# Layers 2 and 3 of a four-layer network: each token's two expert outputs kept as two rows in DRAM, or added into one row by the DMA that sends them

## The chip, the cores and the metric

The kernel runs on one core of one Trainium2 chip, in one launch. The time is device microseconds from the start to the end of an execution, taken as the median of several. The profile shows one further execution with its engines: PE (TensorE, the matrix unit, with PEld its weight loads), DVE (VectorE), ACT (ScalarE), POOL (GpSimd) and SP (SyncE, which here does nothing but issue DMAs). All numbers are fp32.

## The reference

A batch of 4 x 512 = 2048 tokens of 256 features goes through four residual layers. Each layer is an attention-like part plus a feed-forward part, both of the normed (layers 0 to 2) or residual input. In layers 1, 2 and 3 the feed-forward part is a mixture of experts: a router picks a few experts per token, and the token's output is the weighted sum of those experts' outputs. Layer 1 has 32 experts, of which each token uses 4; layer 2 has 7 routed experts, 2 per token, beside a shared one; layer 3 has 8 experts, 2 per token. Cut to what the change touches:

```python
# layer 2 (expert_ffn: silu(x @ wg) * (x @ wu) / 8 @ wd)
scores, idx = jax.lax.top_k(probs, 2)
scores = scores / jnp.sum(scores, axis=-1, keepdims=True)
w = jnp.sum(jax.nn.one_hot(idx, 7) * scores[..., None], axis=-2)
for e in range(7):
    combined = combined + w[..., e:e + 1] * expert_ffn(x, r_gate[e], r_up[e], r_down[e])

# layer 3
top_logits, top_idx = jax.lax.top_k(logits, 2)
cw = jnp.zeros((T, 8)).at[jnp.arange(T)[:, None], top_idx].add(jax.nn.softmax(top_logits, axis=-1))
for e in range(8):
    h = jax.nn.silu(x @ w0[e]) * (x @ w1[e])
    out = out + cw[:, e:e + 1] * (h @ wo[e])

# every layer
x = x + attention(...) + experts(...)
```

The result is x after layer 3.

## The kernel before

The residual stream x stays in SBUF all the time, as 16 tiles of 128 tokens by 256 features. Tensors in DRAM serve only to bring tokens of one expert together and to send them back.

**Routing.** `dispatch` (L158) counts, for each token and expert, which place the token takes among that expert's tokens. Places come in blocks of 128, and a block belongs to one expert: 2048 x 2 / 128 + experts − 1 blocks, so 38 in layer 2 and 39 in layer 3. A block that is not full has empty places. The normed tokens are written to a DRAM tensor `rows`, one row per token: 256 features, the token's number, its two places and its two shares (a row has 272 numbers). `in_slot` names, for every place of every block, the token that stands there.

**A block.** Both layers run over the blocks in a pipeline of stages, each of which handles another block in one turn.

- fetch: SP loads the weights of the block's expert. In layer 3 these are three matrices of 512 KB (`w0`, `w1`, `wo`, 1.5 MB together), in layer 2 one packed piece of 384 KB. POOL issues an indirect DMA, the *gather* (`load_rows`, L294), which brings the 128 rows of the block's tokens to the tile `r`.
- features: `block_rows` (L300 to L317) works out on DVE, for each of the 128 rows, its share and the row it goes to. `mine` (L306) marks which of the token's two places is this one; `both` (L311, L312) is `mine` times the shares and `mine` times 0 or 2048; a reduction (L314) gives the share and the offset; the token's number is added (L315) and the sum is cut at `beyond` (L317), which sends empty places to spare rows. `block_features` turns the rows round on PE (`rt`, L325) and ACT copies them (`rT`, L327).
- hidden: the two matrices of the expert on PE (`g` L1742 in layer 3), Silu on ACT (L1748), the product on DVE (`h` L1749).
- output: the last matrix on PE (`o` L1755 in layer 3, L1107 in layer 2), then `send_back` (L330): ACT scales by the share (`y`, L333), and POOL issues an indirect DMA, the *scatter* (L334), from `y` to the rows `to` of the DRAM tensor `outs`.

`outs` has one row per token and choice: rows 0 to 2047 for the first choice, 2048 to 4095 for the second, then 128 spare rows per block. No row is written twice, and `no_order` (L276) tells the scheduler that these scatters need no order among themselves. So a scatter waits for its data and for a free place in its queue, not for other scatters to land.

**Collecting.** `collect` (L338) adds the outputs to x. For each of 8 pairs of token tiles it loads 256 KB for the first choice and 256 KB for the second (L345 with `load`, L356) and adds both on DVE (L351). These loads wait for all scatters to have landed. In layer 3 the stores of x to the output (`store_x`, L369) follow pair by pair, and the kernel ends with them. Layer 1 uses the same functions with four outputs per token.

**What sets the order.** The engines run their instructions in the order in which a scheduler put them at build time; POOL, SP and DVE each have one queue in order. In layer 2 the experts are worked off beside the gated attention: the last 8 of 32 attention units are run with the experts' stages between their steps, and the collecting stands in front of the last unit (L1059). That unit's steps are, in this order, `ke` (L1193), `pok` (L1240), `ok` (L1245), `okt` (L1249) with `mx`, `pv` on DVE and ACT (L1253 to L1256), `st` (L1189), `Wg` (L1216), and `pvt` (L1269). Layer 3 begins with its norms (`layer_norm3`, L1758) and routers, which need the collected x. Layer 3's attention is mixed into the first blocks of its experts; PE's order there is written out by hand. In the steady part of layer 3's experts, POOL's queue holds alternately the scatter of block t and the gather of block t+6.

**Start-up.** `expert_rows` (L140) makes `rows` and `outs` while the first weights are loaded on SP's queue.

Of the kernel before, what the change touches and what calls it, by code (L numbers as in the profile page):

```python
# [7 lines left out]
F32 = mybir.dt.float32  # L8
AF = mybir.ActivationFunctionType
ALU = mybir.AluOpType  # L10
AX = mybir.AxisListType
PSUM = bass.MemoryType.PSUM

P = 128
NB = 4
T = 512
D = 256
KD = D // P
NTILE = NB * T // P
# [23 lines left out]
class Ring:  # L43
# [17 lines left out]
    def tile(self, shape, dtype, tag, name, bufs=None):  # L61
        if tag not in self.places and self.pool is None:
            n = 1
            for d in shape[1:]:
                n *= d
            self.places[tag] = [self.base[:, self.free + i * n : self.free + (i + 1) * n] for i in range(bufs)]
            self.free += bufs * n
            assert self.free <= self.base.shape[1]
        if tag not in self.places:
            return self.pool.tile(shape, dtype, tag=tag, name=name, **({"bufs": bufs} if bufs else {}))  # L70
        i = self.turn.get(tag, 0)
        self.turn[tag] = i + 1
        ap = self.places[tag][i % len(self.places[tag])][: shape[0], :]
        if len(shape) == 3:
            ap = ap.rearrange("p (a b) -> p a b", b=shape[2])
        return ap


class Net:
# [57 lines left out]

    def expert_rows(self, name, experts, k, sent=False):  # L140

        blocks = NB * T * k // P + experts - 1
        rows = self.tc.dram_tile([blocks * P if sent else NB * T + 1, EXT], F32, name=f"{name}_rows")
        outs = self.tc.dram_tile([k * NB * T + blocks * P, D], F32, name=f"{name}_outs")
        if sent:
            self.load(
                rows.rearrange("(n p) d -> p n d", p=P), self.none.unsqueeze(1).to_broadcast([P, blocks, EXT])  # L150
            )
        else:
            self.load(rows[NB * T :, :], self.none[:1, :])
        return dict(
            name=name, experts=experts, ne=max(experts, 8), k=k, blocks=blocks, rows=rows, outs=outs, sent=sent
        )

    def dispatch(self, moe, rows, top, w, wk, pool, tag, keep=None):  # L158
# [104 lines left out]
    def experts_of_blocks(self, moe, end, tile, keep):  # L263

        nc = self.nc
        ne, k, blocks = moe["ne"], moe["k"], moe["blocks"]
        past, of = tile("past", blocks, ne), tile("of", blocks, 1, of=keep)
        nc.vector.tensor_scalar(past, end[:blocks, :], self.number[:blocks, 0:1], None, ALU.is_le)
        nc.vector.tensor_reduce(of, past, AX.X, ALU.add)
        nc.vector.tensor_scalar(of, of, float(moe["experts"] - 1), None, ALU.min)  # L270
        moe["of"], moe["expert"] = of, tile("expert", blocks, 1, dt=mybir.dt.int32, of=keep)
        nc.vector.tensor_copy(moe["expert"], of)
        moe["beyond"] = tile("beyond", P, blocks, of=keep)
        nc.vector.tensor_scalar(moe["beyond"], self.number[:, :blocks], float(k * NB * T), None, ALU.add)

    def no_order(self, group, inst):  # L276
# [23 lines left out]
    def block_rows(self, moe, t, n, r, wk):  # L300

        nc = self.nc
        k = moe["k"]

        mine = wk.tile([P, n, k], F32, tag="mine", name="mine")
        nc.vector.tensor_tensor(  # L306
            mine, r[:, :, D + 1 : D + 1 + k], self.number[:, t : t + n].unsqueeze(2).to_broadcast([P, n, k]),
            ALU.is_equal,
        )
        both = wk.tile([P, 2, n, k], F32, tag="both", name="both")  # L310
        nc.vector.tensor_tensor(both[:, 0], mine, r[:, :, D + 1 + k : D + 1 + 2 * k], ALU.mult)  # L311
        nc.vector.tensor_tensor(both[:, 1], mine, self.layers[:, :k].unsqueeze(1).to_broadcast([P, n, k]), ALU.mult)  # L312
        share = wk.tile([P, 2, n], F32, tag="share", name="share", bufs=8)
        nc.vector.tensor_reduce(share, both, AX.X, ALU.add)  # L314
        nc.vector.tensor_tensor(share[:, 1], share[:, 1], r[:, :, D], ALU.add)  # L315
        to = wk.tile([P, n], mybir.dt.uint32, tag="to", name="to", bufs=8)
        nc.vector.tensor_tensor(to, share[:, 1], moe["beyond"][:, t : t + n], ALU.min)  # L317
        return share[:, 0], to

# [10 lines left out]
    def send_back(self, moe, ps, to, share, wk):  # L330
        nc = self.nc
        y = wk.tile([P, D], F32, tag="y", name="y", bufs=5)
        nc.scalar.activation(y, ps, AF.Copy, scale=share)  # L333
        self.no_order(moe["name"] + " back", nc.gpsimd.indirect_dma_start(  # L334
            out=moe["outs"][:, :], out_offset=bass.IndirectOffsetOnAxis(ap=to, axis=0), in_=y, in_offset=None
        ))

    def collect(self, moe, wk):  # L338

        for i in range(0, NTILE, 2):  # L340
            x = self.x[:, i : i + 2, :]
            ys = []
            for m in range(moe["k"]):
                y = wk.tile([P, 2, D], F32, tag="sum", name="sum", bufs=8)
                s = (m * NTILE + i) * P  # L345
                self.load(y, moe["outs"][s : s + 2 * P, :].rearrange("(n p) d -> p n d", p=P))
                ys.append(y)
            if len(ys) > 2:
                self.nc.gpsimd.tensor_tensor(ys[0], ys[0], ys.pop(), ALU.add)
            for y in ys[1:] + ys[:1]:  # L350
                self.nc.vector.tensor_tensor(x, x, y, ALU.add)  # L351
# [124 lines left out]
    def layer0(self):  # L476
        nc, a = self.nc, self.a
# [9 lines left out]
        with ExitStack() as ctx:  # L487
            tp = lambda n, bufs, **k: ctx.enter_context(self.tc.tile_pool(name=n, bufs=bufs, **k))
            wp, wk = tp("l0w", 1), tp("l0", 2)
# [10 lines left out]
            rows = wp.tile([P, 10, D], F32, tag="rows", name="rows")  # L500
# [14 lines left out]
            self.l1w = self.router1(32, routing)  # L515
            self.moe1 = self.expert_rows("l1", 32, 4, sent=True)
            self.packed_experts(self.moe1, "l1_w_gate", "l1_w_up", "l1_w_down")
            self.moe2, self.moe3 = self.expert_rows("l2", 7, 2), self.expert_rows("l3", 8, 2)
            self.packed_experts(self.moe2, "l2_r_gate", "l2_r_up", "l2_r_down")
            self.latent_ahead(early)  # L520
            self.weights = {0: self.gated_weights(0)}
# [101 lines left out]
            for b in range(NB):  # L623
                for c, g in enumerate(gates[b]):
# [5 lines left out]
                    for p in range(2):  # L630
                        y = g[:, p, :]
# [1327 lines left out]
```

## Time and profile before

| | |
|---|---|
| median of 3 runs | 2320.91 us (2320.03 to 2325.61) |
| profiled execution | 2334.37 us |
| its span | 2332.6 us |
| mean TensorE clock granted | 0.909 |
| PE busy | 2019.1 us (87%) |
| PE weight loads | 1501.4 us (64%) |
| DVE busy | 1240.0 us (53%) |
| ACT busy | 841.1 us (36%) |
| POOL busy | 625.8 us (27%) |
| scatters (L334), all layers | 172, 980 ns of POOL each |
| gathers (L294), layers 2 and 3 | 77, 1001 ns of POOL each |
| DMA over the span | 244.02 MB, mean 105 GB/s |

The profile page gives busy times over the whole span and in 40 equal slices; the trace behind it answers for any stretch of time what each engine did and what it waited for. A line such as `2245.14 0.99 POOL L334 DMA_INDIRECT l_outs<-y,to` reads: start and duration in us, engine, line of the kernel, operation, output and inputs; what stands in brackets is how long the engine had been idle before, and who ended that. For a DMA the duration on POOL or SP is that of issuing it; its data land later. `l_outs` stands for the `outs` of any layer, `we` for expert weights. Names like `xn<-l_outs` in the tail are the collecting loads of layer 3, into a buffer that is called `xn` there (`sum` in layer 2). The median of runs is 13.5 us below the profiled execution.

### The profile page before, as it was taken

Reading aid. Unit: us, or ns where it says so; the run is one execution under the profiler, and the core shown is the slowest. Engines: PE = TensorE matmul, PEld = TensorE weight load, DVE = VectorE, ACT = ScalarE, POOL = GpSimd, SP = SyncE. Lnnn points to the kernel's source line nnn. Section 1 sums busy time; section 2 is a strip of 40 time slices with the busy share of each in tenths; the row PEclk is TensorE's granted clock in tenths of the full one; section 3 lists DMA queues with packets and bytes.
Section 4 is the critical chain, followed back from the end, with each engine's and each line's share of the span. In section 5 each row is a group of like instructions: output and inputs, shape, how many; then the busy total and the mean of one; then the engine's idle time right before and its main releaser. Section 6 shows DMA issues by size and latency. Waiting matters only on the chain.

```text
span 2332.6 us, 36307 instructions
## 1 busy us (share of the span) xinstructions
PE 2019.1 (87%) x13455; PEld 1501.4 (64%) x13455; DVE 1240.0 (53%) x3682; ACT 841.1 (36%) x1729; POOL 625.8 (27%) x737
## 2 busy tenths in 40 slices
PE   6754088874999999999999999999999968899995
PEld 2453077762566676666766676656778755678995
DVE  5765056657655655565565656546555564422223
ACT  1110056552334443343344444332354413344221
POOL 5334634443111121111111121110444332012331
PEclk8855599996999999999999999998999977899998
DMA  9911378874000000000000000001433220166897
GB/s 314 331 42 58 108 271 280 281 255 146 1 8 10 6 12 6 5 17 6 4 14 5 8 10 5 8 10 39 133 113 110 86 79 19 61 224 237 291 330 242
DMA packets 152536, 244.02 MB, mean 105 GB/s; under 512 B 15846, under 2 KB 111944, under 8 KB 152232
## 3 DMA queue, kind: packets, MB, share of 16 engines
q1 hardware_dynamic: 137336, 199.50, 26.3%
q0 software_dynamic: 15024, 42.20, 5.2%
q8 instruction: 107, 1.75, 0.3%
q14 instruction: 69, 0.57, 0.1%
HBM read 190.41 MB, written 66.58 MB: 110 GB/s over the span
## 4 chain that ended last, share of the span: by engine, by line
PE 64%; DVE 12%; issue 10%; DMA 6%; POOL 5%; ACT 3%; SPq 1%; another core or an unknown queue 0%; POOLq 0%; DVEq 0%; ACTq 0%
PE pt L1216 7%; PE pj L1138 6%; PE g L1742 5%; PE o L1329 4%; PE kq L1551 3%; PE sc L1201 3%; PE pov L1280 2%; PE gu L959 2%; PE o L1755 2%; DMA r<-l_rows,in_slot 2%; PE qk L1519 2%; DVE junk L1526 2%; PE pv L1567 2%; DMA r<-l_rows 2%; PE qkp L1804 1%
## 5 line engine op out<-in xcount | busy, mean ns | idle before, releaser
L334 POOL DMA_INDIRECT l_outs<-y,to x172 | 168.5, 980 | 325.5 <-ACT y L333 243.2
L306 DVE TENSOR_TENSOR mine<-r,number 128x2 f32<-128x2 f32 (+1 forms) x96 | 15.5, 161 | 273.9 <-DMA r<-l_rows,in_slot 207.2
L294 POOL DMA_INDIRECT r<-l_rows,in_slot x77 | 77.1, 1001 | 276.9 <-PE rt L325 147.0
L1742 PEld LDWEIGHTS g<-rT,we 128*128 128x128 f32 x1248 | 145.2, 192 | 5.2 <-ACT rT L327 3.4
L1742 PE MATMUL g<-rT,we 128*128 128x128 f32 x1248 | 145.9, 275 | 2.4 <-ACT rT L327 2.4
L1526 DVE CUSTOM_DVE_ANT_0 junk<-qk,hide 128x512 f32<-128x512 f32 (+3 forms) x256 | 124.7, 487 | 43.5 <-PE qk L1519 24.9
L1559 POOL TENSOR_SCALAR_AFFINE_SELECT pr<-pr 128x512 f32<-128x512 f32 x64 | 40.2, 639 | 339.3 <-ACT pr L1556 339.3
L959 PE MATMUL gu<-rT,we 128*128 128x128 f32 x760 | 112.5, 287 | 21.4 <-issue 9.7
L325 PE MATMUL rt<-ident,r 128*128 128x128 f32 x344 | 67.1, 295 | 70.2 <-DMA r<-l_rows 69.0
L327 ACT COPY rT<-rt 128x256 f32<-128x256 f32 x172 | 62.6, 372 | 178.3 <-PE rt L325 103.1
L1329 PE MATMUL o<-Wo,oT 128*128 128x256 f32 x512 | 126.2, 390 | 0.0
L959 PEld LDWEIGHTS gu<-rT,we 128*128 128x128 f32 x760 | 104.3, 198 | 33.7 <-issue 16.3
L1216 PE MATMUL pt<-Wg,xnT 128*128 128x256 f32 x512 | 124.2, 394 | 1.3 <-PE ot L1322 0.5
L333 ACT ACTIVATE y<-o,share 128x256 f32<-128x256 f32 x172 | 81.2, 473 | 114.9 <-PE o L1755 48.1
L1207 DVE TENSOR_TENSOR s<-sc,keep 128x512 f32<-128x512 f32 x128 | 82.5, 684 | 72.4 <-PE sc L1201 72.3
L1216 PE MATMUL pt<-Wv,xnT 128*128 128x256 f32 x512 | 120.1, 385 | 0.0
L1151 DVE RECIPROCAL rz<-rz 128x128 f32<-128x128 f32 x128 | 117.5, 935 | 0.4
L1216 PEld LDWEIGHTS pt<-Wg,xnT 128*128 128x128 f32 x512 | 97.0, 195 | 26.0 <-issue 7.1
L413 PE MATMUL tr<-ident,xn 128*128 128x128 f32 x160 | 33.7, 357 | 85.8 <-DVE xn L398 81.3
L1216 PEld LDWEIGHTS pt<-Wv,xnT 128*128 128x128 f32 x512 | 95.0, 191 | 15.1 <-DVE st L387 0.2
L1556 ACT ACTIVATE pr<-kq 128x512 f32<-128x512 f32 (+1 forms) x192 | 86.2, 530 | 50.1 <-PE kq L1551 49.5
L325 PEld LDWEIGHTS rt<-ident,r 128*128 128x128 f32 x344 | 53.9, 203 | 77.6 <-issue 75.0
(457 smaller groups left out, 4565.1 us busy)
## 6 DMA issues: line engine op xcount, KB each, us to landing
we<-l_packed SPq DMA_DIRECT2D x133, 384.0 KB
we<-l_w SPq DMA_DIRECT2D x78, 512.0 KB
we<-l_wo SPq DMA_DIRECT2D x39, 512.0 KB
l_rows<-none SPq DMA_DIRECT2D x1, 12920.0 KB
r<-l_rows SPq DMA_DIRECT2D x19, 680.0 KB
xn<-l_outs SPq DMA_DIRECT2D x32, 256.0 KB
l_rows<-xn SPq DMA_DIRECT2D x8, 544.0 KB
l_packed<-l_w_gate SPq DMA_DIRECT2D x1, 4096.0 KB
```

What stands on the lines that cost most here:

```text
L325: nc.tensor.transpose(pt[:, k, :], r[:, :D].rearrange("p (d k) -> p k d", k=KD)[:, k, :], self.ident)
L333: nc.scalar.activation(y, ps, AF.Copy, scale=share)
L334: self.no_order(moe["name"] + " back", nc.gpsimd.indirect_dma_start(out=moe["outs"][:, :], out_offset=bass.IndirectOffsetOnAxis(ap=to, axi ...
L959: nc.tensor.matmul(ps[:, q, :], we[:, q, k * P : (k + 1) * P], rT[:, k, :], start=(k == 0), stop=(k == KD - 1))
L1138: nc.tensor.matmul(ps, w[n][:, k, :], self.xnT[:, k, t["b"] * T : (t["b"] + 1) * T], start=(k == 0), stop=(k == KD - 1))
L1151: inverse = lambda c: nc.vector.reciprocal(rz[:, c * P : (c + 1) * P], rz[:, c * P : (c + 1) * P])
L1207: nc.vector.tensor_tensor(s, ps[hh], keep4, ALU.mult)
L1216: nc.tensor.matmul(ps[:, i, :], self.xnT[:, k, s : s + P], w[n][:, k, :], start=(k == 0), stop=(k == KD - 1))
L1329: nc.tensor.matmul(ps[:, p, :], of_parity(oT[:, h, c * D : (c + 1) * D], p), wo[:, h, :], start=(h == 0), stop=(h == 1),)
L1526: nc.vector.tensor_tensor_reduce(out=junk[:, :m], in0=tiles[j][:, off : off + m], in1=self.hide[:, T - m :], op0=ALU.add, op1=ALU.max, sca ...
L1556: nc.scalar.activation(pr[:, j, off : off + m], tiles[j][:, :m], AF.Exp, scale=0.25)
L1742: nc.tensor.matmul(pt[:, m, :], we[:, q, k * T + m * P : k * T + (m + 1) * P], rT[:, k, :], start=(k == 0), stop=(k == KD - 1),)
```

## The change

For layers 2 and 3, `outs` has one row per token (2048) and 128 spare rows, in place of two rows per token and 128 spare rows per block. Two DMAs on SP's queue in the start-up fill each of these tensors, 2.23 MB, with zeros. The scatter becomes an indirect DMA that adds `y` to what the row holds. A token's row is now written by two scatters, and all blocks share the spare rows, so the scatters are no longer declared free of order: the scheduler puts a wait for the landing of the one before into each. The row to send to is the token's number itself, so two of the six DVE operations per block are gone. The collecting loads one tile per pair in place of two, and adds it: 8 loads and 8 additions in place of 16 and 16, in each of the two layers. Layer 1 stays as it was.

```diff
-    def expert_rows(self, name, experts, k, sent=False):
+    def expert_rows(self, name, experts, k, sent=False, added=False):
...
-        outs = self.tc.dram_tile([k * NB * T + blocks * P, D], F32, name=f"{name}_outs")
+        outs = self.tc.dram_tile([NB * T + P if added else k * NB * T + blocks * P, D], F32, name=f"{name}_outs")
+        if added:
+            n = NB * T // P + 1
+            self.load(
+                outs.rearrange("(n p) d -> p n d", p=P), self.hide[:, :D].unsqueeze(1).to_broadcast([P, n, D])
+            )
...
         moe["beyond"] = tile("beyond", P, blocks, of=keep)
+        if moe["added"]:
+            nc.vector.tensor_copy(moe["beyond"], self.number[:, NTILE : NTILE + 1].to_broadcast([P, blocks]))
+            return
...
+        share = wk.tile([P, 2, n], F32, tag="share", name="share", bufs=8)
+        to = wk.tile([P, n], mybir.dt.uint32, tag="to", name="to", bufs=8)
+        if moe["added"]:
+            nc.vector.tensor_tensor(mine, mine, r[:, :, D + 1 + k : D + 1 + 2 * k], ALU.mult)
+            nc.vector.tensor_reduce(share[:, 0], mine, AX.X, ALU.add)
+            nc.vector.tensor_tensor(to, r[:, :, D], moe["beyond"][:, t : t + n], ALU.min)
+            return share[:, 0], to
...
         nc.scalar.activation(y, ps, AF.Copy, scale=share)
+        if moe["added"]:
+            nc.gpsimd.indirect_dma_start(
+                out=moe["outs"][:, :], out_offset=bass.IndirectOffsetOnAxis(ap=to, axis=0), in_=y, in_offset=None,
+                compute_op=mybir.AluOpType.add,
+            )
+            return
...
-            for m in range(moe["k"]):
+            for m in range(1 if moe["added"] else moe["k"]):
...
-            self.moe2, self.moe3 = self.expert_rows("l2", 7, 2), self.expert_rows("l3", 8, 2)
+            self.moe2, self.moe3 = self.expert_rows("l2", 7, 2, added=True), self.expert_rows("l3", 8, 2, added=True)
```

More of the change, by code (lines that the diff above doesn't have):

```diff
@@ L154, in expert_rows @@
         return dict(
-            name=name, experts=experts, ne=max(experts, 8), k=k, blocks=blocks, rows=rows, outs=outs, sent=sent
+            name=name, experts=experts, ne=max(experts, 8), k=k, blocks=blocks, rows=rows, outs=outs, sent=sent,
+            added=added,
         )
@@ L312, in block_rows @@
         nc.vector.tensor_tensor(both[:, 1], mine, self.layers[:, :k].unsqueeze(1).to_broadcast([P, n, k]), ALU.mult)
-        share = wk.tile([P, 2, n], F32, tag="share", name="share", bufs=8)
         nc.vector.tensor_reduce(share, both, AX.X, ALU.add)
         nc.vector.tensor_tensor(share[:, 1], share[:, 1], r[:, :, D], ALU.add)
-        to = wk.tile([P, n], mybir.dt.uint32, tag="to", name="to", bufs=8)
         nc.vector.tensor_tensor(to, share[:, 1], moe["beyond"][:, t : t + n], ALU.min)
```

## Prediction

> **What bounds the kernel now.** I read the page first: its rows in 40 slices (58.3 us each) for PE, DMA engines and GB/s.
>
> ```profile
> PE   6754088874999999999999999999999968899995
> ...
> DMA  9911378874000000000000000001433220166897
> GB/s 314 331 42 58 108 271 280 281 255 146 1 8 10 6 12 6 5 17 6 4 14 5 8 10 5 8 10 39 133 113 110 86 79 19 61 224 237 291 330 242
> ```
>
> PE is full nearly throughout; from slice 36 on the DMA engines are nearly full beside it, and in the last slice PE stops and DMA goes on. The busy time by stretches says the same (columns: stretch, its length, PE, PEld, DVE, ACT, POOL busy, PE clock, DMA share, GB/s):
>
> ```profile
> 1880.00:1935.00 55.00, 30.23 (x177) 24.02 (x175) 34.46 (x80) 9.62 (x18) 22.83 (x33) 0.75 0.26 80
> 2178.00:2290.00 112.00, 112.00 (x854) 107.87 (x853) 30.00 (x140) 29.30 (x61) 38.73 (x40) 1.00 0.99 330
> 2310.00:2333.00 23.00, 0.00 (x0) 0.00 (x0) 11.07 (x16) 0.00 (x0) 0.00 (x0) 0.50 0.80 274
> ```
>
> The change touches three places: the boundary after layer 2's experts (PE 30 of 55 us), layer 3's experts (PE 112 of 112, DMA 0.99), and the tail (no PE at all). The waits of the middle stretch show what each engine waits for (us in total, times, longest):
>
> ```profile
> DVE mine L306 <- DMA r<-l_rows,in_slot: 79.2, 20, 5.9
> POOL r L294 <- PE rt L325: 43.8, 19, 2.3
> POOL l_outs L334 <- ACT y L333: 28.8, 20, 4.5
> ```
>
> POOL issues a scatter and a gather per block, waiting for other engines, never for a landing. The timeline of one block, then of the tail (start, duration):
>
> ```profile
> 2244.38 0.86 SPq L356 DMA_DIRECT2D we<-l_w  x2
> 2244.39 0.47 ACT L333 ACTIVATE y<-o,share 128x256 f32<-128x256 f32 x1 [1.30 <-PE o L1755]
> 2245.14 0.99 POOL L334 DMA_INDIRECT l_outs<-y,to  x1 [1.28 <-ACT y L333]
> 2245.42 0.38 SPq L356 DMA_DIRECT2D we<-l_wo  x1
> ...
> 2248.43 0.97 POOL L294 DMA_INDIRECT r<-l_rows,in_slot  x1 [2.31 <-PE rt L325]
> ...
> 2250.68 0.99 POOL L334 DMA_INDIRECT l_outs<-y,to  x1 [1.27 <-ACT y L333]
> ...
> 2305.80 0.97 POOL L334 DMA_INDIRECT l_outs<-y,to  x1 [4.33 <-ACT y L333]
> 2306.82 0.47 ACT L333 ACTIVATE y<-o,share 128x256 f32<-128x256 f32 x1 [1.30 <-PE o L1755]
> 2307.57 0.97 POOL L334 DMA_INDIRECT l_outs<-y,to  x1 [0.81 <-ACT y L333]
> 2310.33 11.42 SPq L356 DMA_DIRECT2D xn<-l_outs  x16
> ```
>
> Scatters come every 5.54 us, each 0.76 us behind a burst of 1.5 MB of weights. The chain that ended last gives the last scatter's landing, with no weights beside it:
>
> ```profile
> 2307.57 2.40 DMA l_outs<-y,to
> 2313.88 5.53 DMA xn<-l_outs
> ```
>
> By the trace's landing records a scatter takes 2.63 us to its last landing in layer 2 (median), but 6.94 in 2178–2290, first landing at 5.2; the gather 3.3 us later takes 5.30. So 6.94 exceeds the 5.54 of a block: today two scatters overlap, which costs nothing.
>
> **What the Trainium skill says.** "DMA: Bandwidth & Descriptors", "Rules for kernel authors": an accumulating DMA reads its destination and writes it later, so another access of the same bytes must wait for the earlier DMA's semaphore. The changed program does: each adding scatter waits for the one before to land. The trace of before has no such DMA. "Issuing engines are not separate DMA queues" puts all transfers on the same 16 engines; the trace agrees (2.40 us alone, 6.94 beside weights). "Latency and other measured facts" gives an HBM access 0.2 us on average and 2 us at high load; I use it as the bound for the added read, which no trace here shows. "SBUF — State Buffer", "Who interferes with whom", has two-input DVE operations contend with GpSimd's reads: an x add beside POOL's x took 2.08 us, alone 0.66.
>
> **The change part by part**, against the profiled execution (2334.4 us; the median of runs is 13.5 less, and I carry that difference over).
>
> Tail of layer 3: removed are 8 of 16 loads of 256 KB and 8 of 16 DVE adds. From the first load's issue at 2310.33 to the last store's landing at 2331.46 is 21.1 us, for 4.19 MB loaded and 2.10 stored. About 2 us of it is the first landing's delay; the other 19.1 scale with bytes, 6.29 to 4.19 MB: 12.7. **−6.4 us.** The adds (0.71 us each) keep ahead of the loads either way.
>
> The last two scatters: issued 1.77 us apart, while the first lands after 2.40. The second must slip 0.65 if an added row costs nothing, 1.6 or more if it costs 1. **+1.1**, and the last one's own extra landing 0.2 to 2, **+0.5** (an added read without load lies near the lower end).
>
> Boundary of layer 2: collect starts at S = 1881.42 after the last landing, +0.5 for the adding. It has 8 loads and adds fewer. But the order of DVE changes: before, the second `ke` and `ok` (L1245) came after two adds, ending S+5.3; after, they come behind all eight adds and the norms of b = 0, 1, which wait for POOL's `rs`. Eight adds and those norms put `ok`'s end at S+18.8 to S+21.7 (0.68 to 1.1 us an add, two rounds through POOL of about 3 us). Behind `ok` PE has 9.3 us up to the end of `Wg`, then `pvt` (L1269), today at S+28.5 after waiting 14.0 us for `pv`. `pv` follows `ok` on DVE without the adds now, so break-even is `ok` at S+19.2: −0.4 to +2.5. With the later start **+1.7**.
>
> Layer 3's experts: one new wait per block. Behind a scatter held back on POOL stands the next gather; a block later `mine` (L306) waits for it on DVE, behind `mine` the `h` of the block before (L1749), and for `h` PE's `o`. The slack: POOL idles 2.3 us ahead of each gather, and `h` is done 3.9 us before PE takes it (at 2266.26 for 2270.14), 6.2 in all. At today's phase a scatter needs 6.94 for a 5.54 us block, so the first slips 1.4, the next again, until they stand later against the burst; at the gather's phase (3.3 later) a transfer needs 5.30. I expect the phase to lock there, inside the slack: **+0.5**. The added read of 0.131 MB is 128 packets of 1 KB at 46 ns (the trace's) over 16 engines, 0.37 us of every engine per block, 0.64 if the destination's packets are also written as 1 KB. Over 20 blocks that is 7 to 13 us of DMA backlog in a stretch already at 0.99; w0 and w1 land by about 7.5 us and are needed after about 16.6, 9 us of cover: 0 to +3, **+1**.
>
> Early layer 3 (gaps of 2.57 and 3.2 us between scatters, at 2085, 2098 and 2113): up to 1 us a pair, gathers behind them are on the chain there: **+0.5** (0 to 3). Layer 2's few close pairs lie under a full PE: 0.
>
> DVE: two of six small operations fewer in each of 77 blocks, 0.16 us each, hidden beside PE; `to` comes 0.35 us earlier ahead of `h`: **−0.5** (−2 to 0). Start-up: two fills of 2.23 MB are put on SP's queue ahead of layer 2's packed weights; at 350 GB/s they take 12.7 us, and the DMA engines idle from 136 to 198 us, and what stands behind the fills on SP serves layer 2: 0, and without that cover up to 13. An adding scatter may take POOL longer to issue than 0.98 us; twice that is still hidden by the 2.3.
>
> Sum: −6.4 + 1.1 + 0.5 + 1.7 + 0.5 + 1.0 + 0.5 − 0.5 = −1.6, so 2332.8, or **2319 us** as median.
>
> **Rivals.** A, the chain of landings becomes the bound (slower). Place: 2178–2300, 21 scatters. If an adding scatter takes more than 5.54 + 6.2/21 = 5.84 us in its best phase, PE waits for POOL. For it: 5.30 is the best phase for a gather, and a read at high load may add up to 2. Against: a longer block thins the weights and shortens the landing. At 6.5: 21 × 0.96 − 6.2 = +14, about 2333; at 7.3, +31, about 2350.
>
> B, all gains are felt (faster): the 8 adds fewer at the boundary (8 × 0.68 = 5.5 us) bring `pvt` about 3 forward, because norms don't hold up `ok`; DVE gives 1, the pair costs 0.65, the rest nothing: −6.4 − 3 − 1 + 0.65 = −9.8, 2311. Against it stands the order of DVE.
>
> C, the DMA engines are the bound: the added traffic at 0.64 to 1 us a block uses up the 9 us of cover, 20 × 0.64 − 9 = +4 to 20 × 1 − 9 = +11 beyond my sum's other terms (−2.6): 2322 to 2329.
>
> **How the numbers follow.** Forecast 0.41 (own range 2312 to 2327), A 0.27, B 0.20, C 0.12. A difference of 0.3% (7 us, so 2313.9 and 2327.9) is about what a measurement of this kernel tells from none. Faster: 0.19 of B and 0.05 of the forecast, 0.24. Slower: 0.26 of A, 0.06 of C, 0.02 of the forecast, 0.34. Within: 0.42. The range 2311 to 2345 leaves out half of B (0.10) and the worst of A (0.09).
>
> **What would show it.** Right: tail from first load to end about 15 us; scatters in 2178–2300 still 5.54 apart, waiting for a landing, later against the weights, PE above 99%; POOL's wait for landings as a new row of waits; `ok` after all adds. Wrong: scatters 6 us or more apart with PE waiting for `rt` (A); PE waiting for weights, DMA 1.0 (C); `pvt` earlier than S+26 (B). An adding scatter that lands unloaded in 5 us or more, or a POOL issue beyond 3 us, upsets the terms everywhere.

## The result and the profile after

The changed kernel takes 2339.28 us (median of 4 runs, 2335.07 to 2344.26) against 2320.47 for the kernel before, a ratio of 1.0087 with an interval of 1.0060 to 1.0114: 18.8 us slower. A second set of five runs gave 1.0100 (1.0084 to 1.0117).

The page's rows in 40 slices (58.6 us each now) for PE, DMA engines and GB/s, of the kernel after:

```profile
PE   6754188857999999999999999999999858999985
...
DMA  9931488872000000000000000003444311377996
GB/s 318 344 99 65 147 276 283 303 246 73 1 12 10 6 12 6 8 10 5 8 10 5 13 5 5 12 5 108 105 102 109 67 50 39 120 221 220 294 274 176
```

In the kernel before PE was full up to the last slice but one (9), and the DMA engines moved 237, 291, 330 and 242 GB/s in the last four slices; now that slice is an 8, and they move 220, 294, 274 and 176. The same work is spread over more time. The busy time of layer 3's experts and of the tail (columns as in the prediction; the tail's stretch begins 10 us later than there):

```profile
2178.00:2290.00 112.00, 101.38 (x714) 95.02 (x713) 18.08 (x80) 24.51 (x51) 41.19 (x32) 0.95 0.94 282
...
2320.00:2343.00 23.00, 0.00 (x0) 0.00 (x0) 5.45 (x8) 0.00 (x0) 1.55 (x1) 0.50 0.63 194
```

Layer 3's experts were a stretch in which PE worked all the time (112.00 of 112); now PE works 101.38 of it, at a mean granted clock of 0.95 in place of 1.00, and starts 714 matmuls where it started 854. The waits of that stretch name what holds whom (us in total, times, longest):

```profile
DVE mine L315 <- DMA r<-l_rows,in_slot: 89.7, 16, 7.2
...
POOL l_outs L349 <- DVE mine L322: 19.4, 5, 5.1
POOL l_outs L349 <- DMA l_outs<-y,to: 18.2, 4, 5.8
PEld o L1775 <- DVE h L1769: 12.3, 9, 2.5
```

The second and the third line are the same wait: a scatter on POOL waits for its data and for the landing of the scatter before, and the view names whichever event stands last in its records. That it is the landing shows in POOL's timeline:

```profile
2190.64 1.59 POOL L349 DMA_INDIRECT l_outs<-y,to  x1 [5.83 <-DMA l_outs<-y,to]
2192.54 0.99 POOL L303 DMA_INDIRECT r<-l_rows,in_slot  x1 [0.30 <-PE rt L339]
2197.97 1.59 POOL L349 DMA_INDIRECT l_outs<-y,to  x1 [4.45 <-DMA l_outs<-y,to]
2199.86 0.99 POOL L303 DMA_INDIRECT r<-l_rows,in_slot  x1 [0.30 <-issue]
2203.97 1.59 POOL L349 DMA_INDIRECT l_outs<-y,to  x1 [3.12 <-DVE mine L315]
```

By the landing records the scatter of 2190.64 landed after 6.56 us, at 2197.20, and the next one started 0.77 later; that one landed at 2203.20, and the next started again 0.77 later. The difference between the distance of two scatters and the landing of the first is 0.73 to 0.82 us in 32 of layer 3's 38 intervals; in the other six, all among the first 13, it is 2.66 us or more. The gather, which used to have 2.3 us of POOL's time ahead of it, now follows its scatter after 0.30: it is late with it, `mine` waits for the gather, `h` stands behind `mine`, and PE waits for `h` (fourth line above). The mean distance of the scatters from the 15th to the 34th is 6.81 us, where it was 5.54.

The chain that ended last shows the end of the layer:

```profile
2309.66 3.64 DMA l_outs<-y,to
...
2314.12 3.57 DMA l_outs<-y,to
...
2318.45 3.58 DMA l_outs<-y,to
...
2322.78 3.73 DMA l_outs<-y,to
...
2329.12 5.97 DMA xn<-l_outs
```

PE's last matmul ends at 2314.6 and the last `y` is ready at 2315.1, but two scatters still stand in line, and the last is issued 7.7 us later. An adding scatter lands in 3.6 us where a plain one took 2.4. Half of the difference is on POOL, by the list of the tensor's instructions (duration in ns, shortest, median, longest):

```profile
L354 POOL DMA_INDIRECT l_outs<-y,to x95: 954/960/1921, 294.1 to 507.8; - x95
L349 POOL DMA_INDIRECT l_outs<-y,to x77: 1552/1586/1654, 1631.4 to 2322.8; - x77
```

The first line is layer 1's plain scatters, the second the adding ones. The packet records agree: of the scatter of 2305.80 in the kernel before, the first packet starts 1.55 us after POOL does and the packets take 0.51 us from the first start to the last end; of that of 2318.45 in the kernel after it is 2.13 and 1.10.

Where the time went, from the scatters' starts in the two profiled executions:

| stretch | before | after | difference |
|---|---|---|---|
| layer 2, first to last scatter | 232.9 | 236.5 | +3.6 |
| last of layer 2 to first of layer 3 | 193.5 | 190.2 | −3.3 |
| layer 3, first to last scatter | 235.2 | 264.7 | +29.6 |
| last scatter to the end of the span | 25.0 | 19.7 | −5.3 |

These add up to +24.5 us before rounding. The two spans differ by 9.9 only, because the execution of before was slower ahead of layer 2: its last scatter of layer 1 stands at 523.2, that of after at 507.8. Both values occur with the same code in that part (the runs below, none of which changes layers 0 and 1 beyond the fills, have 507 to 512 on one chip and 520 to 526 on the two others), so this goes with the chip and not with the change, and I leave it out. Over all profiles, the first difference lies within what the same code gives: in the nine in which layer 2 is plain, its stretch takes 232.8 to 237.6 us. The boundary takes 191.9 to 193.9 us in those nine and 189.2 to 190.9 in the three where layer 2 adds, so its gain stands out. The stretch of layer 3 takes 234.7 to 235.2 us in the three in which layer 3 is plain, and 262.3 to 264.9 in the four in which it adds into one tensor beside all its weights.

### The profile page after: what moved, and what is told of

It is laid out like the page before. It is cut to its first block, busy times and chain, and to the rows that moved or that the text cites. A ratio compares the mean times of both kernels' runs of the same rounds, so it can differ in the third digit from the quotient of the medians.

```text
span 2342.5 us, 36056 instructions
## 1 busy us (share of the span) xinstructions
PE 2016.9 (86%) x13455; PEld 1498.7 (64%) x13455; DVE 1198.6 (51%) x3512; ACT 842.1 (36%) x1731; POOL 675.6 (29%) x737
## 4 chain that ended last, share of the span: by engine, by line
PE 57%; DMA 12%; DVE 9%; issue 7%; ACT 4%; POOL 3%; SPq 0%; POOLq 0%; DVEq 0%; ACTq 0%
PE pt L1236 8%; PE pj L1158 6%; DMA l_outs<-y,to 6%; PE o L1349 4%; DMA r<-l_rows,in_slot 3%; PE sc L1221 3%; PE kq L1571 3%; PE pov L1300 3%; PE gu L979 2%; PE qk L1539 2%; DMA r<-l_rows 2%; DVE junk L1546 2%; PE pv L1587 2%; PE g L1762 2%; PE qkp L1824 1%
## 5 line engine op out<-in xcount | busy, mean ns | idle before, releaser
L349 POOL DMA_INDIRECT l_outs<-y,to x77 | 121.9, 1583 | 239.8 <-ACT y L347 90.8
L354 POOL DMA_INDIRECT l_outs<-y,to x95 | 95.9, 1009 | 132.9 <-ACT y L347 83.9
```

Source lines behind the costliest of these rows:

```text
L349: nc.gpsimd.indirect_dma_start(out=moe["outs"][:, :], out_offset=bass.IndirectOffsetOnAxis(ap=to, axis=0), in_=y, in_offset=None, compute_ ...
```

## The experiments

Theory T: each scatter waits for the landing of the one before, and this chain bounds layer 3 (the prediction's rival A). Rival U: the adding costs, by POOL's issue and the DMA engines' time, wherever it stands. Each ratio is against runs of the kernel before on the same chip; that kernel's median was 2333.3 us beside the runs with either layer alone, with the wait alone and with two tensors, 2332.0 beside the two of the last experiment, and 2318.4 beside the others. A loss in us is the ratio's distance from 1 times that median. Expected times in us were written with 2320 us for the kernel before.

### Either layer alone

```diff
-            self.moe2, self.moe3 = self.expert_rows("l2", 7, 2, added=True), self.expert_rows("l3", 8, 2, added=True)
+            self.moe2, self.moe3 = self.expert_rows("l2", 7, 2, added=True), self.expert_rows("l3", 8, 2)
```

and the other way round.

> Only layer 2 adds in DRAM; layer 3 sends two rows per token as before. Theory T (the chain of landings in layer 3's experts is what costs): layer 2's experts lie under a full PE, so the wait costs a few us there and the boundary gives 3 back; 2316 to 2325 us, within 0.3% of before. Rival U (the adding itself costs wherever it stands, by POOL's longer issue and the DMA engines' time): layer 2 carries half of the loss, 2328 to 2332 us.

> Only layer 3 adds in DRAM. Theory T: it carries the whole loss, 2338 to 2346 us, scatters about 6.7 us apart in the stretch where they stood 5.54 apart, and queued up at the end 4.4 apart. Rival U: half of the loss, 2328 to 2332 us.

Layer 2 alone: 0.9996 (0.9987 to 1.0004). Layer 3 alone: 1.0123 (1.0108 to 1.0137), 28.7 us, with scatters 6.87 us apart from the 15th to the 34th and 4.5 at the end. All of the loss is layer 3's, so U is out in its plain form. In layer 2 the same scatters land in 3.81 us (median), their blocks stand 6.4 us apart on average, more than 3.81 + 0.77, and PE has attention to compute beside them. From its first to its last scatter that layer takes 235.7 us in the profile of the first of these runs, and 234.3 and 232.8 in those of layer 3 alone and of the wait alone, where layer 2 is plain.

### The changed kernel once more

> The changed kernel once more, beside the same runs of before as the three below. If the parts add up, the ratio is that of layer 2 alone times that of layer 3 alone, 0.9996 x 1.0123 = 1.012; if adding in both layers gives something that neither part alone gives (the boundary between them starts earlier, say), it is about 1.009 again.

1.0100 (1.0084 to 1.0117). The product of the parts, 1.012, has an interval of its own of about 0.0016 to each side, so this doesn't decide between 1.009 and 1.012: the parts add up within what the runs can tell.

### The wait without the adding

The kernel before, its layer 3 scatters no longer declared free of order:

```diff
-        self.no_order(moe["name"] + " back", nc.gpsimd.indirect_dma_start(
+        sent = nc.gpsimd.indirect_dma_start(
             out=moe["outs"][:, :], out_offset=bass.IndirectOffsetOnAxis(ap=to, axis=0), in_=y, in_offset=None
-        ))
+        )
+        if moe["name"] != "l3":
+            self.no_order(moe["name"] + " back", sent)
```

> The kernel before, with two rows per token and plain scatters, but each scatter of layer 3 waits for the landing of the one before, as the adding ones do. Theory T: the wait is the cause, the adding makes it longer. A plain scatter lands about 1.2 us earlier than an adding one, so 5.5 to 6.1 us apart in the busy stretch and 3.2 at the end: 2327 to 2336 us, half or more of the loss without the tail's gain. Rival U: a wait alone is hidden as it was forecast, 2319 to 2324 us.

1.0055 (1.0042 to 1.0069), 12.8 us. The wait alone costs, as T says, but less than the half of the loss that was expected: without the tail's gain (8.4 us, measured below) layer 3 alone loses some 37 us, an estimate from 28.7 + 8.4, and 12.8 is a third of it. POOL's timeline at the end of the layer, of this run:

```profile
2299.39 0.97 POOL L334 DMA_INDIRECT l_outs<-y,to  x1 [2.20 <-DMA l_outs<-y,to]
2302.68 0.97 POOL L334 DMA_INDIRECT l_outs<-y,to  x1 [2.33 <-DMA l_outs<-y,to]
2305.88 0.97 POOL L334 DMA_INDIRECT l_outs<-y,to  x1 [2.22 <-DMA l_outs<-y,to]
2309.05 0.97 POOL L334 DMA_INDIRECT l_outs<-y,to  x1 [2.21 <-DMA l_outs<-y,to]
```

A queue of plain scatters empties at 3.2 us each: 2.42 for the landing and 0.77 to the next start. In the busy stretch they land in 5.28 (median) and stand 5.85 apart on average, and PE works nearly all the time:

```profile
2178.00:2290.00 112.00, 111.46 (x846) 107.14 (x846) 28.50 (x135) 29.17 (x61) 38.03 (x39) 1.00 0.98 330
```

So the phase did move as I had foreseen, from 6.94 to 5.28, but the 0.77 was not in my sum. One reservation: the profiled execution was the fastest of six of this kernel (2335.93 us, of 2335.93 to 2350.44), and in it layer 3 takes only 3.5 us more from its first to its last scatter than the plain layer 3 of the run with layer 2 alone. Where the slower executions lose the rest isn't shown.

### The adding with twice the time

Layer 3 alone adds, even blocks into one tensor, odd blocks into another:

```diff
-                out=moe["outs"][:, :], out_offset=bass.IndirectOffsetOnAxis(ap=to, axis=0), in_=y, in_offset=None,
+                out=moe["outs"][t % 2][:, :], out_offset=bass.IndirectOffsetOnAxis(ap=to, axis=0), in_=y, in_offset=None,
                 compute_op=mybir.AluOpType.add,
```

with two fills, and collecting loads from both tensors.

> Only layer 3 adds, but even and odd blocks add into two DRAM tensors, so that a scatter waits for the landing of the one before last; collecting loads two tiles as before. The adding, its longer issue and its traffic stay, the chain has twice the time. Theory T: PE is back at 5.54 us per block, 2319 to 2326 us. Rival U (traffic and issue cost): the loss of the run with one tensor stays, 2335 us or more.

1.0006 (0.9998 to 1.0014). The busy stretch of this run:

```profile
2178.00:2290.00 112.00, 112.00 (x852) 107.80 (x851) 22.42 (x97) 29.23 (x61) 51.47 (x40) 1.00 1.04 329
```

PE is back at 112.00, the scatters at 5.53, although each lands in 7.63 us there (median), still takes POOL 1.58 to issue, and the DMA share is above that of before. The adding's own cost, with its traffic, is 1.4 us, at most 3.3 by the interval. So neither the adding without the chain (1.4) nor the chain without the adding (12.8) makes the 37 us: the chain is the cause, and most of the loss comes from the adding's making each of its turns longer.

### What makes the landing long

Layer 3 alone adds, and of a block's weights only `w0` is loaded; it stands in for `w1`, and one matrix, loaded once, for every `wo`:

```diff
-        for q, n in enumerate(("w0", "w1")):
-            self.load(we[:, q], a["l3_" + n][bass.ds(e, 1)].rearrange("o (p k) n -> p (o k n)", k=KD))
-        self.load(
-            we[:, 2].rearrange("p (k n) -> p k n", k=4),
-            a["l3_wo"][bass.ds(e, 1)].rearrange("o (k p) n -> p (o k) n", p=P),
-        )
+        self.load(we[:, 0], a["l3_w0"][bass.ds(e, 1)].rearrange("o (p k) n -> p (o k n)", k=KD))
...
```

> Layer 3 alone adds in DRAM as in the run l3_only, but of each block's 1.5 MB of weights only w0 is loaded; w0 stands in for w1, and the last matrix is that of expert 0 for all blocks, so layer 3's experts compute something else with as many matmuls. If the weights' traffic is what makes a landing 6 us long, it falls to 3.8 to 4.5, a scatter is due 4.6 to 5.3 after the last, PE returns to 5.54 us per block, and the run takes 25 us or more less than l3_only, no slower than before. If the landing is long by the adding itself, it stays near 6 and the run near l3_only's time.

0.9992 (0.9983 to 1.0001), where layer 3 alone with all weights has 1.0123. Stretch of this run:

```profile
2178.00:2290.00 112.00, 112.00 (x854) 107.87 (x853) 23.07 (x92) 29.11 (x61) 49.29 (x38) 1.00 0.55 129
```

The adding scatters land in 3.85 us, the next one starts 1.68 us after the landing, 0.9 more than the chain needs, and PE works all the time. So a turn of the chain in the kernel after is 3.8 us of the scatter itself, some 2 us of standing among weights, and 0.77.

### Gathers ahead of the chain

Layer 3 alone adds, and every gather is issued two blocks earlier into five buffers, by two more stages at the front of the pipeline:

```diff
-                stages = self.fetch3, self.features3, self.hidden3, lambda t, we, *state: state, self.output3
+                ahead = lambda t, we, *state: state
+                stages = self.rows3, ahead, self.fetch3, self.features3, self.hidden3, ahead, self.output3
...
```

> Layer 3 alone adds in DRAM as in l3_only, but every gather is issued two blocks earlier, into five buffers in place of three. If the loss comes from the gather that stands behind a waiting scatter, two blocks (11 us) of further slack per gather bring PE back for a good part of the stretch and the ratio falls from 1.0123 to 1.007 or less. If the chain of landings is the bound itself, POOL still passes one scatter per landing, the backlog shows up behind PE's end, and the ratio stays at 1.010 to 1.013.

1.0113 (1.0094 to 1.0132): not better than 1.0123 beyond the intervals. The scatters stand 6.72 apart, and in 31 of the 38 intervals the next one starts about 0.77 us (0.73 to 0.82) after the landing. At the end of this run:

```profile
2309.59 3.62 PE L1780 MATMUL o<-we,h 128*128 128x256 f32 x16
...
2317.09 1.55 POOL L349 DMA_INDIRECT l_outs<-y,to  x1 [2.93 <-DMA l_outs<-y,to]
2321.65 1.55 POOL L349 DMA_INDIRECT l_outs<-y,to  x1 [3.02 <-DMA l_outs<-y,to]
```

PE runs at its own 5.53 in the last blocks, the last four intervals of the scatters are 4.5 to 4.6 us, and the last scatter starts 8.4 us after PE has finished. Slack for the gather moves part of the stall to the end and doesn't remove it.

### The tail alone

The kernel before, its last collecting without the second choice's loads and additions (`choices` is 1 in layer 3):

```diff
-            for m in range(moe["k"]):
+            for m in range(choices or moe["k"]):
...
```

> The kernel before, but the collecting of layer 3 leaves out the second choice: 8 loads and 8 additions in place of 16 and 16, so the second experts' outputs are missing from the result. It measures the tail's gain alone. My sum says 6.4 us faster, ratio 0.9972; a rival (loads that were hidden behind stores and additions) says 0 to 2 us.

0.9964 (0.9951 to 0.9977), 8.4 us faster (5.3 to 11.4); my 6.4 lies within the interval. In this run's profile the last scatter stands at 2288.5 and the span ends at 2306.9, 18.4 us, where it was 25.0: 6.6 us.

### The tail's gain without the chain

Layer 3's first 35 blocks send as in the kernel before, and their 16 loads and additions are put beside the last four blocks; only these four add, into a tensor of their own, and the tail loads that. In the second version PE also takes the last matrix of block 37 ahead of block 38.

```diff
+        if moe["late_outs"] is not None and t >= moe["late"]:
+            nc.gpsimd.indirect_dma_start(
+                out=moe["late_outs"][:, :], out_offset=bass.IndirectOffsetOnAxis(ap=to, axis=0), in_=y, in_offset=None,
+                compute_op=mybir.AluOpType.add,
+            )
+            return
...
+                    if n == moe["blocks"] + 1:
...
+                        self.collect(moe, sums)
...
-            self.collect(moe, Ring(self.rows.rearrange("p i d -> p (i d)"), self.small, {"sum": (8, 2, D)}))
+            self.collect_last(moe, sums)
...
```

> A way to have the shorter tail without the chain: in layer 3 the first 35 of 39 blocks send as before (two rows per token, no order; the rows are filled with zeros in the start-up), and their 16 collecting loads run while the last four blocks compute, where the DMA engines are nearly idle. Only the last four blocks add, into a tensor of one row per token, so the tail loads 8 tiles. The tail gains the 8.4 us that the run tail_half measured; the last scatter must wait for the one before it and lands 4 to 4.5 us later than in the kernel before. Ratio 0.9965 to 0.9995, 4 us faster. If the early loads or additions get in the way of the last blocks, no gain: 1.000 or more.

> As l3_late_sum, and PE multiplies the last matrix of the block before the last ahead of the last block's first matrices, so that the last two scatters are due about a block apart. The last block's end moves back by 1.9 us less what was lost to waiting; the last scatter lands about 1 us earlier than in l3_late_sum: ratio lower by 0 to 0.0005.

1.0008 (0.9998 to 1.0019) and 1.0007 (0.9997 to 1.0017): no gain, against what was expected. From the last scatter to the end the first run takes 19.6 us in place of 25.0, but layer 3 takes 242.8 from its first to its last scatter in place of 235.2. Its timeline at the end:

```profile
2301.07 1.99 POOL L353 DMA_INDIRECT l_late<-y,to  x1 [3.92 <-ACT y L351]
...
2309.27 1.88 POOL L353 DMA_INDIRECT l_late<-y,to  x1 [6.20 <-DMA l_late<-y,to]
2309.63 0.68 DVE L1786 TENSOR_TENSOR h<-g,h 128x512 f32<-128x512 f32 x1
2310.23 4.67 DVE L382 TENSOR_TENSOR x<-x,xnT 128x512 f32<-128x512 f32 x7
2310.36 3.78 PE L1792 MATMUL o<-we,h 128*128 128x256 f32 x8 [4.78 <-DVE h L1786]
```

Two things took the gain. The early additions stand ahead of the last `h` on DVE, wait for their loads, and PE waits 4.78 us for `h`. And the early loads do to the scatter of 2301.07 what the weights do: the next one could start only 8.2 us later. The second version shows both again: PE waits 3.95 us for `h`, and the scatter after that of 2298.80 starts 8.9 us later. Neither version beats the kernel before.

## Why the prediction was wrong

The forecast was 2319 us; measured were 2339. The time is within what rival A gave (2333 to 2350), and slower was what I held for less likely than no difference (0.34 against 0.42).

**The step that failed** is "I expect the phase to lock there, inside the slack: +0.5" for layer 3's experts. Measured from the first to the last scatter of that layer: +29.6 us, of which 19 × (6.81 − 5.54) = 24 from the 15th to the 34th. The path was the one I had named, a scatter held back and behind it the gather, `mine`, `h` and PE; that it would stay inside the slack was wrong. I had compared a landing (5.30 in its best phase) with a block (5.54). Three things were missing:

- The next scatter starts 0.77 us after the landing; I had put this at nothing. With it, even a plain scatter would need 5.30 + 0.77 = 6.07, above the 5.84 that I had worked out as the point from which A decides. Measured in the run with the wait alone was a turn of 5.85, just at that point, in an execution in which PE lost 0.5 us of the stretch; by the ratio of all its runs the loss is 12.8.
- An adding scatter takes POOL 1.59 us. I had set "twice that is still hidden by the 2.3" against POOL's idle time; but it lies inside the chain from landing to landing, where nothing hides it. It is 0.6 of the 1.2 us by which an adding scatter lands later, as the start of the first packet shows (2.13 us against 1.55).
- The other 0.6 us is in the DMA. I had 0.2 to 2 from the Trainium skill's HBM latencies ("DMA: Bandwidth & Descriptors", "Latency and other measured facts") and took the low end for an unloaded landing; for the last scatter of all the landing is 3.73 against 2.40, so the term of 0.5 in the tail was 1.3. For a block of layer 3 I had added no such time to the landing at all.

Summed, 5.30 + 0.77 + 1.2 = 7.3; measured were 6.81. That a slower block thins the weights, as I had argued against A, fits this (282 GB/s in the stretch in place of 330), but no run separates it.

The other steps:

- **Tail**, −6.4: right. From the first collecting load to the end of the span it was 22.2 us and is 15.9; the run with the tail alone gives 8.4 ± 3.
- **Last two scatters**, +1.1: too small. They came out of a queue that had built up, the last one 7.7 us after its data; before, 0.3. Without a queue it is too small as well: in the run that loads `w0` alone the last two stand 4.57 us apart, 2.8 more than in before.
- **Boundary**, +1.7: the order of DVE did what was said: `ok` ended 18.98 us after the first load (18.8 to 21.7), and `pvt` stood at +27.1 where it had been at +28.5, so that the start, later by 1.4 us after the last scatter, was just made good. But the whole boundary came out at −3.3, which none of my terms gives: after `pvt` the matmuls ran faster. 16 of `sc` and 8 of `o`, which follow it, took 2.08 and 3.61 us in before, right behind a wait of PE of 14 us, and 1.16 and 2.00 in after, where PE's long wait (13 us, for `ke`) ends 9.5 us ahead of `pvt`. The clock records go with this: in before the granted clock is 0.50 from 1900.04 to 1917.10, up to 7.2 us after the start of `pvt`; in after it is back at 1.00 from 1895.68, 3.1 us ahead of `pvt`. The two groups make 2.5 of the 3.3 us. I had not looked at the clock that PE is granted after a wait.
- **DMA backlog**, +1, and rival C: the added traffic is larger than I took. The queue of POOL's DMAs has 5.2% of 16 engines' span before and 7.6% after, (178 − 121) / 77 = 0.74 us per adding scatter, where I had 0.37 to 0.64. It is 128 packets of 1 KB in place of 32 of 4 KB, and such a packet takes 102 ns (median), not the 46 of a loading packet that I used. Still the run with two tensors has PE full at a DMA share of 1.04, so C is out at this size.
- **Early layer 3**, +0.5 (0 to 3): from the first to the 15th scatter 106.3 us before and 110.9 after, +4.6.
- **Layer 2's close pairs**, 0: +3.6 between its first and last scatter, within what the same code varies by; 0.9996 in all.
- **DVE and start-up**, −0.5 and 0: no loss that the runs can tell; the two-tensor run has two fills and 1.0006.

Rival A is what happened, with one correction: it had PE wait for `rt`, and PE waited for `h`. Rival B is out: its gain at the boundary came in size (−3.3 for −3), but by luck, since `pvt` stood at S+27.1 and not before S+26; the tail's gain came too, and the chain took both several times over.

## What to carry to other kernels

A scatter that adds where a scatter used to write turns independent transfers into a chain, and what counts is then the whole turn: POOL's issue, the landing under the traffic that is there, and the time from the landing to the next start. Compare that turn, not the landing, with the time per block; a landing that took longer than a block, and overlapped the next one at no cost, was the sign here. If the turn is too long, a second tensor for every other block gives each chain twice the time, but here that gave back just what the adding was to save.

## What was not expected of the hardware

From the last landing of an indirect DMA to the start of the next one that waits for it on POOL, 0.77 us pass (0.73 to 0.83 in five runs, plain and adding alike). SP started the collecting loads sooner, 0.02 us after layer 2's last landing and 0.05 to 0.37 after layer 3's. An adding scatter of 128 rows of 1 KB takes POOL 1.58 us to issue in place of 0.96, lands in 3.6 to 3.8 us with little beside it in place of 2.4 to 2.6, and moves in 128 packets in place of 32.

In these traces the longer waits of PE cost more than themselves. The same eight matmuls of layer 3's `o` take 1.9 to 2.0 us when PE has waited up to 1.7 us just before them; behind the three waits of 1.8 to 2.3 us in 2178–2300 of the kernel after they take 2.8 to 3.4, and behind the waits of 3.95 and 4.78 us in the two runs of the last experiment 3.45 and 3.78. In the stretch of the kernel after the clock records show 0.50 three times for 3.41 us each, from 2219.94, 2240.42 and 2281.38, while these slower matmuls run, and 1.00 elsewhere. The page counts a slow matmul as busy PE, so 101.38 of 112 us busy was 714 matmuls of 854.
